# Turning attention outputs into columns on VectorE instead of TensorE, squaring on ScalarE, and three moved steps

## The chip, the cores and the metric

The kernel runs on one core of a Trainium2 chip. The metric is the device time of one execution in microseconds (us). Engines are named as in the profile: PE is TensorE (PEld its weight loads), DVE is VectorE, ACT is ScalarE, POOL is GpSimd, SP is SyncE, which issues most DMAs. Each engine works through its own queue in order, and waits at an instruction whose inputs are not there yet.

## The reference

The input `x` is 8 batches x 512 features x 1024 tokens, float32; a 0/1 mask says which tokens of a batch are kept. Eight heads of 64 features attend, with one projection for queries, keys and values, and the result is added to `x`:

```
xt = transpose(x, (0, 2, 1)); q = xt @ Wq.T              # per head: dk = 64
logits = (scale * q q^T * cmask + (1 - cmask) * -1e30) * rmask
attn = softmax(logits); ctx = attn @ q
out = transpose(ctx @ Wo.T, (0, 2, 1))
return x + out
```

A query that is masked has all its logits at 0, so it gets the mean over all tokens, which is the same for all masked queries.

## The kernel before

About half the tokens are kept. The kernel counts each batch's kept tokens and, if all have fewer than NK = 576, gathers them (and one row with the mean) into 576 columns, attends among those alone, multiplies by Wo, and spreads the rows back to 1024 tokens by an indirect DMA. A second path for all tokens stands behind a branch and does not run here.

**Tiles.** Features are cut into 4 pieces of 128 (a piece is two heads); a batch and a piece make a pair, so there are 8 x 4 = 32 pairs, `p` = 4b + pr. Keys are cut into 5 chunks (four of 128, one of 64). The main loop in `late` runs over pairs and in each over the chunks c = 0..4; such a step is called a slot (pr, c) here. The order of all engines' work is written out by hand: what a slot calls is recorded in that order, and each engine takes its instructions in it.

**A slot** does `scores` (PE: L625, two halves of two matmuls, PSUM tiles `s` in two buffers; ACT: the exponential L629 of each half), `add_up` of the chunk before (DVE: L646, sums over valid keys), then what the dictionaries and `slots_of` put there. After slot 4 comes `attend` (PE: L662, 40 matmuls; ACT copies the result, L678). Two pairs ahead, `project` (PE L556, 4 matmuls per half; ACT copy L563) and `values` (PE transposes L575, ACT copy L578, then DVE: square L583, sum by head L585, maximum L592) prepare queries and values. `bias_of` (L598) puts the maximum into a row with one PE product, reduces it on DVE (L600) and makes the bias that the next pair's exponentials need. It stands in slot 1. `contexts` (DVE, L750 to L759) scales a pair's result by inverse sums that went through DRAM (`row`, `rb`).

**Output of batch b.** During pair (b+1, 1), `output` (PE L775, ACT L782) multiplies by Wo in five pieces, put in slots 0, 1, 1, 2 and 3, and POOL stores them to DRAM (`od`, L784). `load_rest` in slot (1, 2) loads `x` again, as 8 tiles `xr` of 128 features x 512 tokens. `fetch` in slot (2, 0) has POOL gather rows of `od` by `origin` into 8 tiles `g` of 128 tokens x 512 features (L846). `finish`, two calls in each of the slots (3, 1) to (3, 4), makes 4 PE transposes (L858) into one PSUM bank and adds that to `xr` on DVE (L861); `issue_stores` issues the stores a slot later on SP (L863). The finish of batch 6 stands behind all of batch 7, and batch 7 itself has its own (`fetch_last` L835, `finish_tokens` L872, L873).

**Next batch's input.** In the slots (0, 2), (0, 4), (1, 0), (1, 1) DVE turns 32x32 blocks of the next `x` (L445; tiles `xt` in two buffers), and SP stores them as `xd` in DRAM (L453, four DMAs of 32 partitions each). `search` (L500) finds the kept tokens, `gather` in slot (1, 3) fetches them on POOL (L512), `collect` in slots (2, 2) and (2, 3) transposes them on PE (L525). `load_batch` in (3, 0) loads the batch after that.

**PSUM.** Two buffers of two banks hold `s`; every other product takes one of four banks in turn (`bank`), so a product waits until the reader of the fourth product before it is done.

Of the kernel before, what the change touches and what calls it, by code (L numbers as in the profile page):

```python
# [10 lines left out]
F32 = mybir.dt.float32  # L11
I32 = mybir.dt.int32
AF = mybir.ActivationFunctionType
ALU = mybir.AluOpType
# [7 lines left out]
Q = 32  # L22
# [296 lines left out]
def attention_of_kept_tokens(ctx, tc, x, mask, wq, wo, out, ident, wqT, woT, verdict, flag):  # L319
# [43 lines left out]
    sb = ctx.enter_context(tc.tile_pool(name="fsb", bufs=2))  # L363
# [7 lines left out]
    key = keep.tile([P, NC], F32, name="key")  # L371
    kept = keep.tile([P, B], F32, name="kept")
    origin = keep.tile([P, B, NT], I32, name="origin")
    pads = keep.tile([P, B, NC], F32, name="pads")
    pens = keep.tile([P, B, NC], F32, name="pens")
    low = keep.tile([P, 2, LAST], F32, name="low")
# [5 lines left out]
    def bank(name):  # L382
        return ps.tile([P, NB], F32, tag="t", name=name, bufs=4)
# [4 lines left out]
    stores = [[], []]  # L388
# [178 lines left out]
    def values(pair):  # L567
        nm = "%d_%d" % pair
        qT = qTs[pair]
        v = sb.tile([P, NC, P], F32, tag="v", name=f"v_{nm}", bufs=4)  # L570
        for at, n in ((0, LAST), (LAST, 1)):
            pt = bank(f"v_{nm}_{at}")
            for i in range(n):
                c = at + i
                nc.tensor.transpose(  # L575
                    pt[:, i * P : (i + 1) * P], qT[:, c * P : (c + 1) * P], ident
                )
            nc.scalar.copy(  # L578
                v[:, at : at + n, :], pt[:, : n * P].rearrange("p (c d) -> p c d", d=P)
            )  # L580
        vs[pair] = v
        sq = sb.tile([P, NC, P], F32, tag="sq", name=f"sq_{nm}", bufs=1)
        nc.vector.tensor_tensor(sq, v, v, ALU.mult)  # L583
        lengths = sb.tile([P, 2 * NC], F32, tag="len", name=f"len_{nm}")
        nc.vector.tensor_reduce(  # L585
            lengths,
            sq.rearrange("p c (h d) -> p (c h) d", h=2),
            axis=AX.X,
            op=ALU.add,
        )  # L590
        tops[pair] = sb.tile([P, 1], F32, tag="top", name=f"top_{nm}")
        nc.vector.tensor_reduce(tops[pair], lengths, axis=AX.X, op=ALU.max)  # L592
# [213 lines left out]
    def end_output(b, i):  # L806
# [12 lines left out]
        nc.vector.tensor_tensor(oc[:n, :], po[:n, :], partials[i][:n, :], ALU.add)  # L819
        nc.sync.dma_start(ods[b][places[i], :], oc[:n, :])  # L820

    def load_rest(b):
        for r in range(NN):
            for d in range(ND):
                xr = sb.tile([P, NB], F32, tag="xr", name=f"xr_{b}_{r}_{d}", bufs=NN * ND)
                nc.sync.dma_start(xr, x[b, d * P : (d + 1) * P, r * NB : (r + 1) * NB])
                xrs[b, r, d] = xr

    def fetch_last(b):

# [12 lines left out]
    def fetch(b):  # L843
        for i in range(NT):
            g = sb.tile([P, D], F32, tag="g", name=f"g_{b}_{i}", bufs=NT)
            nc.gpsimd.indirect_dma_start(  # L846
                out=g,
                out_offset=None,
                in_=ods[b],
                in_offset=bass.IndirectOffsetOnAxis(ap=origin[:, b, i : i + 1], axis=0),  # L850
            )
            gs[b, i] = g

    def finish(b, r, d):
        xr = xrs.pop((b, r, d))
        pt = bank(f"o_{b}_{r}_{d}")
        for i in range(G):
            nc.tensor.transpose(  # L858
                pt[:, i * P : (i + 1) * P], gs[b, r * G + i][:, d * P : (d + 1) * P], ident
            )  # L860
        nc.vector.tensor_tensor(xr, pt, xr, ALU.add)  # L861
        stores[0].append(
            lambda: nc.sync.dma_start(out[b, d * P : (d + 1) * P, r * NB : (r + 1) * NB], xr)  # L863
        )

    def finish_tokens(b, i):

# [18 lines left out]
    def slots_of(p):  # L886

        b, pr = pairs[p]
        todo = [[] for _ in range(NC)]
        if p + 2 < len(pairs):  # L890
            ahead = pairs[p + 2]
            at = (4, 4) if p == 2 else (3, 4) if pr == 2 else (1, 3) if p == 0 else (0, 2)
            for hf in range(2):
                todo[at[hf]].append(lambda hf=hf: project(ahead, hf))
            todo[LAST].append(lambda: values(ahead))
        if p == 0:
            behind = pairs[1]
            todo[0].append(lambda: project(behind, 1))
            todo[1].insert(0, lambda: values(behind))
            todo[3].insert(0, lambda: bias_of(behind))  # L900
        if p == ND - 1:
            for d in range(ND):
                todo[1 + d].append(lambda d=d: turn_weights(woT, "wo", d))
        if pr == 1 and b > 0:
            for i in range(NC):
                todo[(0, 1, 1, 2, 3)[i]].append(lambda i=i: output(b - 1, i))
        if pr == 2 and b + 1 < B:
            todo[1].append(lambda: put_mean(b + 1))
            for i in reversed(range(NC)):
                todo[(2, 2, 2, 3, 3)[i] + (b == 0)].insert(0, lambda i=i: collect(b + 1, i))  # L910
        if pr == 3 and 0 < b < B - 1:
            for i in range(NN * ND):
                r, d = divmod(i, ND)
                todo[1 + i // 2].append(lambda r=r, d=d: finish(b - 1, r, d))
        if p + 1 == len(pairs):
            for i in range(NC):
                todo[(1, 1, 2, 3, 4)[i]].append(lambda i=i: begin_output(b, i))
        return todo
# [29 lines left out]
    def early():  # L948
# [105 lines left out]
            search(0, i)  # L1054
        pt = bank("home_t")
        nc.tensor.transpose(pt[:, :BC], home, ident[:BC, :BC])
        nc.vector.tensor_copy(origin, pt[:, :BC].rearrange("p (b c) -> p b c", c=NT))

    def late():
        weights["wq"] = order_columns(load_weights(wq, "wq"), "wq")  # L1060
# [19 lines left out]
        TURN = [(0, 2), (0, 4), (1, 0), (1, 1)]  # L1080
        SEARCH = {(1, 0): (0, 1), (1, 1): (2,), (1, 2): (3,), (1, 3): (4,)}
        LATER = {(1, 1): (0,), (1, 2): (1,), (1, 3): (2, 3), (1, 4): (4,)}
        for p, pair in enumerate(pairs):
            b, pr = pair
            before = pairs[p - 1] if p else None
            todo = slots_of(p)
            for c in range(NC):
                scores(pair, c)
                if c:
                    add_up(pair, c - 1)  # L1090
                if c == 0 and before:
# [11 lines left out]
                if 0 < p < len(pairs) - 1 and c == (3 if p == 2 else 1):  # L1103
                    bias_of(pairs[p + 1])
                if b + 1 < B:
                    if (pr, c) in TURN:
                        turn(b + 1, TURN.index((pr, c)))
                    if pr < 2 and pr * NC + c < NN * ND:
                        add_features(b + 1, pr * NC + c)
                    if pr == 1 and c == 3:  # L1110
                        mean_of(b + 1)
                    for i in (SEARCH if b else LATER).get((pr, c), ()):
                        search(b + 1, i)
                    if pr == 0 and c == 1:
                        queries_of(b + 1)
                    if pr == 1 and c == (3 if b else LAST):
                        for i in range(NC):
                            gather(b + 1, i)
                if pr == 3 and c == 0 and b + 2 < B:
                    load_batch(b + 2)  # L1120
                    load_ranks(b + 2)
                if pr == 1 and c == 2 and b > 0:
                    load_rest(b - 1)
                if pr == 2 and c == 0 and b > 0:
                    fetch(b - 1)
                for task in todo[c]:
# [6 lines left out]
        attend_last(last)  # L1133
        for i in (0, LAST, *range(1, LAST)):
            end_output(B - 1, i)
        for r in range(NN):
            for d in range(ND):
                finish(B - 2, r, d)
                issue_stores()
# [113 lines left out]
```

## Time and profile before

| what | value |
|---|---|
| median of 3 runs | 738.48 us (737.36 to 738.85) |
| the profiled execution | 745.78 us, of which the span from first to last instruction is 744.1 us |
| mean granted PE clock | 0.981 |
| PE busy | 696.8 us (94%) |
| DVE busy | 526.8 us (71%) |
| ACT busy | 363.6 us (49%) |
| POOL busy | 171.0 us (23%) |
| moved by DMA | 117.40 MB, mean 158 GB/s |
| one batch in the middle, from `attend` to `attend` | 85 to 86 us |

The profile gives for each engine the time in which its instructions ran; a share near 100% doesn't say by itself that the engine sets the time. The chain of waits does: it is followed back from the last instruction, at each step to what released it. In the rows of instruction groups, the columns are line, engine, operation, what is written and read, shape, count | busy us in all, mean ns of one | idle us of the engine just before them and what ended it.

### The profile page before, as it was taken

Reading aid. Unit: us, or ns where it says so; the run is one execution under the profiler, and the core shown is the slowest. Engines: PE = TensorE matmul, PEld = TensorE weight load, DVE = VectorE, ACT = ScalarE, POOL = GpSimd, SP = SyncE. Lnnn points to the kernel's source line nnn. Section 1 sums busy time; section 2 is a strip of 40 time slices with the busy share of each in tenths; the row PEclk is TensorE's granted clock in tenths of the full one; section 3 lists DMA queues with packets and bytes.
Section 4 is the critical chain, followed back from the end, with each engine's and each line's share of the span. In section 5 each row is a group of like instructions: output and inputs, shape, how many; then the busy total and the mean of one; then the engine's idle time right before and its main releaser. Section 6 shows DMA issues by size and latency. Waiting matters only on the chain.

```text
span 744.1 us, 12368 instructions
## 1 busy us (share of the span) xinstructions
PE 696.8 (94%) x4251; PEld 405.1 (54%) x4251; DVE 526.8 (71%) x1527; ACT 363.6 (49%) x731; POOL 171.0 (23%) x208
## 2 busy tenths in 40 slices
PE   6799899999999899999999999999999999998983
PEld 5555565456655565456654565555654566554342
DVE  6279868774996569956897759956798668637462
ACT  5466466454553646345464546435473644435300
POOL 4712010161103501044101701044000620014021
PEclk9899999999999999999999999999999999999995
DMA  8544142754557463564738545574736542334047
GB/s 285 174 141 120 43 160 76 229 164 136 188 142 228 154 212 108 148 197 132 244 104 241 164 138 191 137 229 142 245 102 188 174 132 74 88 138 132 0 150 259
DMA packets 80857, 117.40 MB, mean 158 GB/s; under 512 B 10912, under 2 KB 43744, under 8 KB 80784
## 3 DMA queue, kind: packets, MB, share of 16 engines
q1 hardware_dynamic: 64032, 74.14, 32.3%
q0 software_dynamic: 12528, 40.28, 17.1%
q10 hardware_dynamic: 4224, 2.10, 1.0%
q8 instruction: 35, 0.57, 0.3%
q14 instruction: 38, 0.31, 0.1%
HBM read 73.30 MB, written 43.18 MB: 157 GB/s over the span
## 4 chain that ended last, share of the span: by engine, by line
PE 87%; ACT 4%; DVE 4%; DMA 2%; issue 1%; POOL 0%; another core or an unknown queue 0%; ACTq 0%; POOLq 0%; DVEq 0%
PE s L625 20%; PE av L662 20%; PE pq L556 18%; PE po L775 15%; PE o L858 3%; PE v L575 3%; ACT e L629 3%; PE xc L525 3%; PE pa L795 2%; DVE junk L500 1%; DMA g<-od,origin 1%; PE xt L416 1%; PE top L598 1%; DVE junk L646 1%; PE po L811 1%
## 5 line engine op out<-in xcount | busy, mean ns | idle before, releaser
L646 DVE CUSTOM_DVE_ANT_0 junk<-e,valid 128x576 f32<-128x576 f32 x256 | 193.3, 755 | 95.8 <-ACT e L629 90.0
L625 PE MATMUL s<-qT 64*128 64x288 f32 (+1 forms) x1280 | 185.1, 432 | 10.5 <-ACT e L629 10.4
L629 ACT ACTIVATE e<-s,bias 128x576 f32<-128x576 f32 x256 | 176.8, 739 | 35.5 <-PE s L625 30.0
L625 PEld LDWEIGHTS s<-qT 64*128 64x128 f32 (+1 forms) x1280 | 92.3, 174 | 91.9 <-issue 46.4
L556 PE MATMUL pq<-xc,wqT 128*128 128x288 f32 x512 | 140.5, 418 | 1.2 <-issue 1.2
L662 PE MATMUL av<-e,v 128*64 128x288 f32 x1024 | 134.1, 413 | 0.0
L556 PEld LDWEIGHTS pq<-xc,wqT 128*128 128x128 f32 x512 | 92.2, 190 | 42.2 <-issue 12.0
L775 PE MATMUL po<-woT,cT 128*128 128x512 f32 (+1 forms) x336 | 113.2, 523 | 0.0
L662 PEld LDWEIGHTS av<-e,v 128*64 128x64 f32 x1024 | 71.8, 138 | 51.1 <-issue 6.6
L784 POOL DMA_DIRECT2D od<-oc x42 | 24.0, 573 | 264.7 <-ACT oc L782 252.3
L678 ACT COPY cT<-av 128x288 f32<-128x288 f32 x62 | 21.8, 402 | 123.8 <-PE av L662 123.5
L775 PEld LDWEIGHTS po<-woT,cT 128*128 128x128 f32 (+1 forms) x336 | 49.8, 173 | 50.7 <-issue 46.2
L846 POOL DMA_INDIRECT g<-od,origin x56 | 61.8, 1104 | 34.2 <-PE s L625 11.9
L782 ACT COPY oc<-po 128x512 f32<-128x512 f32 (+1 forms) x35 | 19.0, 544 | 84.3 <-PE po L775 80.3
L583 DVE TENSOR_TENSOR sq<-v 128x640 f32<-128x640 f32 x32 | 26.0, 813 | 47.7 <-ACT v L578 46.2
L563 ACT COPY qT<-pq 128x288 f32<-128x288 f32 x64 | 25.6, 399 | 56.2 <-PE pq L556 51.4
L512 POOL DMA_INDIRECT xin<-xd,source x40 | 41.4, 1034 | 47.3 <-DVE cT L759 27.6
L404 POOL TENSOR_SCALAR valid<-count,kept 128x576 f32<-128x576 f32 x8 | 14.3, 1785 | 133.7 <-DVE sums L646 133.5
L861 DVE TENSOR_TENSOR xr<-o,xr 128x512 f32<-128x512 f32 x56 | 35.8, 684 | 7.7 <-PE o L858 7.3
L500 DVE TENSOR_SCALAR_CACHE_REDUCE junk<-rank,key 128x1024 f32<-128x1024 f32 (+4 forms) x40 | 39.7, 993 | 1.8 <-ACT rank L1025 1.8
L464 ACT ACTIVATE junka<-x 128x512 f32<-128x512 f32 x56 | 35.3, 631 | 0.0
L445 DVE STREAM_TRANSPOSE xt<-x 128x1024 f32<-128x1024 f32 x28 | 34.8, 1242 | 0.5 <-issue 0.2
(138 smaller groups left out, 651.4 us busy)
## 6 DMA issues: line engine op xcount, KB each, us to landing
x<-in_x_dram SPq DMA_DIRECT2D x56, 256.0 KB
xd<-xt SPq DMA_DIRECT2D x112, 128.0 KB
xr<-in_x_dram SPq DMA_DIRECT2D x56, 256.0 KB
out_dram<-xr SPq DMA_DIRECT2D x56, 256.0 KB
rb<-row SPq DMA_DIRECT2D x60, 160.0 KB
od<-oc POOLq DMA_DIRECT2D x28, 256.0 KB
rank<-ranks SPq DMA_DIRECT2D x6, 512.0 KB
xd<-xt POOLq DMA_DIRECT2D x8, 256.0 KB
```

The lines of the kernel that those rows point to most:

```text
L445: nc.vector.transpose(xt.rearrange("p k (d f) -> p k d f", d=ND), xs[b][r][:, :, at : at + n].rearrange("p d (k t) -> p k d t", t=Q),)
L464: nc.scalar.activation(junk, xs[b][r][:, d, :], AF.Copy, accum_out=xbars[b][:, d, r : r + 1])
L500: nc.vector.tensor_scalar(junk[:, :n], rank[:, i * P :], key[:, col], 0.0, ALU.is_le, ALU.add, accum_out=found[:, col])
L512: nc.gpsimd.indirect_dma_start(out=xin[:n, :], out_offset=None, in_=xds[b], in_offset=bass.IndirectOffsetOnAxis(ap=searches[b][2][:n, i : ...
L556: nc.tensor.matmul(pq[:, :KH], wqT[:, d, pr * P : (pr + 1) * P], xcs[b][:, d, cols], start=(d == 0), stop=(d == ND - 1),)
L625: nc.tensor.matmul(s[to, h, :KH], qT[heads[h], keys], qT[heads[h], queries], start=True, stop=True)
L629: nc.scalar.activation(e[:, hf if c < LAST else 0, :, :], s[:, :, :KH], AF.Exp, bias=biases[pair][:, c : c + 1], scale=SCALE,)
L646: nc.vector.tensor_tensor_reduce(junk[:, :n].rearrange("p (f k) -> p f k", k=KH), e[:, :, h, :], (valid if c < LAST else part).rearrange(" ...
L662: nc.tensor.matmul(av[head, :KH], v[keys, c, head], e[keys, hf if c < LAST else 0, h, :], start=(c == 0), stop=(c == LAST),)
L775: nc.tensor.matmul(po[k * n : (k + 1) * n, :w], cTs[b, pr][:, i * P : i * P + n], woT[:, pr, k * w : (k + 1) * w], start=(pr == 0), stop=( ...
L846: nc.gpsimd.indirect_dma_start(out=g, out_offset=None, in_=ods[b], in_offset=bass.IndirectOffsetOnAxis(ap=origin[:, b, i : i + 1], axis=0),)
L861: nc.vector.tensor_tensor(xr, pt, xr, ALU.add)
```

## The change

1. **Square.** `sq` in `values` is made by an ACT activation (Square) instead of a DVE product.
2. **Output into columns.** For all batches but the last, `finish` is replaced by `finish_blocks`. `x` and the output are seen as `(k f) (a n) -> a f k n` with f = 32 features and a = 4 quarters of the tokens: partition 32a + f holds the features f, 32 + f, 64 + f, ... of quarter a. `xr` becomes one tile of 128 x 16 x 256 in one buffer, loaded by four DMAs of 32 partitions with runs of 1 KB. Row 32a + t of gathered tile i is token 256a + 32i + t; `block_origin` holds the rows in that order and `place_blocks` makes it once in slot (2, 2) of batch 0, with 16 small DVE copies. `finish_blocks(b, i)` is then one DVE transpose of 32x32 blocks (128 x 512) and one DVE addition in SBUF, into 16 runs of 32. The output is stored by four DMAs, once per batch; for batch 6 in two halves.
3. **Where it stands.** The eight calls are in the slots (2, 3), (2, 4) twice, (3, 0) to (3, 3), and (0, 1) of the batch after; batch 6 has five calls in slots (3, 1) to (3, 3) of batch 7 and three behind it.
4. **Maxima.** `bias_of` moves from slot 1 to the slot of the pair's second projection (slot 2), for pr = 2 from slot 1 to slot 3.
5. **Output products.** The fifth piece of `output` moves from slot (1, 3) to slot (1, 2); so POOL stores it ahead of the five gathers and no longer behind them.

```diff
-        nc.vector.tensor_tensor(sq, v, v, ALU.mult)
+        nc.scalar.activation(sq, v, AF.Square)
...
+    def place_blocks():
+
+        for a in range(A):
+            for j in range(A):
+                nc.vector.tensor_copy(
+                    block_origin[a * Q : (a + 1) * Q, :, j::A],
+                    placed[j * Q : (j + 1) * Q, :, a * (NT // A) : (a + 1) * (NT // A)],
+                )
...
+        xr = sb.tile([P, D // Q, T // A], F32, tag="xr", name=f"xr_{b}", bufs=1)
+        for a in range(A):
+            nc.sync.dma_start(xr[a * Q : (a + 1) * Q, :, :], in_blocks(x[b])[a])
+        xrs[b] = xr
+
+    def finish_blocks(b, i):
+        o = sb.tile([P, D // Q, Q], F32, tag="o", name=f"o_{b}_{i}", bufs=2)
+        nc.vector.transpose(o.rearrange("p k t -> p (k t)"), gs[b, i])
+        xr = xrs[b]
+        to = xr[:, :, i * Q : (i + 1) * Q]
+        nc.vector.tensor_tensor(to, o, to, ALU.add)
+        n = NT if b + 2 < B else G
+        if (i + 1) % n == 0:
+            cols = slice((i + 1 - n) * Q, (i + 1) * Q)
...
+            stores[0].append(store)
...
-    def finish(b, r, d):
-        xr = xrs.pop((b, r, d))
-        pt = bank(f"o_{b}_{r}_{d}")
-        for i in range(G):
-            nc.tensor.transpose(
-                pt[:, i * P : (i + 1) * P], gs[b, r * G + i][:, d * P : (d + 1) * P], ident
-            )
-        nc.vector.tensor_tensor(xr, pt, xr, ALU.add)
...
+            if 0 < p != 2:
+                todo[at[pr != 2]].append(lambda: bias_of(pairs[p + 1]))
...
-                todo[(0, 1, 1, 2, 3)[i]].append(lambda i=i: output(b - 1, i))
+                todo[(0, 1, 1, 2, 2)[i]].append(lambda i=i: output(b - 1, i))
...
+        FINISH = {
+            (2, 3): (0,),
+            (2, 4): (1, 2),
+            (3, 0): (3,),
+            (3, 1): (4,),
+            (3, 2): (5,),
+            (3, 3): (6,),
+            (0, 1): (7,),
+        }
+        FINISH_LAST = {(3, 1): (0, 1), (3, 2): (2, 3), (3, 3): (4,)}
```

More of the change, by code (lines that the diff above doesn't have):

```diff
@@ L373, in attention_of_kept_tokens @@
     origin = keep.tile([P, B, NT], I32, name="origin")
+    placed = keep.tile([P, B, NT], F32, name="placed")
+    block_origin = keep.tile([P, B, NT], I32, name="block_origin")
     pads = keep.tile([P, B, NC], F32, name="pads")
@@ L820, in end_output, with in_blocks, store @@
         nc.sync.dma_start(ods[b][places[i], :], oc[:n, :])
-    def load_rest(b):
[L823 to L827, printed above, removed]
+    BLOCKS = range(B - 1)
+    def place_blocks():
[5 more added lines that the diff above has]
+                )
+    def in_blocks(t):
+        return t.rearrange("(k f) (a n) -> a f k n", f=Q, a=A)
+    def load_rest(b):
+        xr = sb.tile([P, D // Q, T // A], F32, tag="xr", name=f"xr_{b}", bufs=1)
[11 more added lines that the diff above has]
+            cols = slice((i + 1 - n) * Q, (i + 1) * Q)
+            def store():
+                for a in range(A):
+                    nc.sync.dma_start(
+                        in_blocks(out[b])[a][:, :, cols], xr[a * Q : (a + 1) * Q, :, cols]
+                    )
+            stores[0].append(store)
     def fetch_last(b):
@@ L849, in fetch @@
                 in_=ods[b],
-                in_offset=bass.IndirectOffsetOnAxis(ap=origin[:, b, i : i + 1], axis=0),
+                in_offset=bass.IndirectOffsetOnAxis(
+                    ap=block_origin[:, b, i : i + 1], axis=0
+                ),
             )
             gs[b, i] = g
-    def finish(b, r, d):
-        xr = xrs.pop((b, r, d))
-        pt = bank(f"o_{b}_{r}_{d}")
-        for i in range(G):
-            nc.tensor.transpose(
-                pt[:, i * P : (i + 1) * P], gs[b, r * G + i][:, d * P : (d + 1) * P], ident
-            )
[L861 to L864, printed above, removed]
     def finish_tokens(b, i):
@@ L910, in slots_of @@
                 todo[(2, 2, 2, 3, 3)[i] + (b == 0)].insert(0, lambda i=i: collect(b + 1, i))
[L911 to L914, printed above, removed]
         if p + 1 == len(pairs):
@@ L1056, in early @@
         nc.tensor.transpose(pt[:, :BC], home, ident[:BC, :BC])
-        nc.vector.tensor_copy(origin, pt[:, :BC].rearrange("p (b c) -> p b c", c=NT))
+        nc.vector.tensor_copy(placed, pt[:, :BC].rearrange("p (b c) -> p b c", c=NT))
+        nc.vector.tensor_copy(origin, placed)
     def late():
@@ L1102, in late @@
                     contexts(before)
-                if 0 < p < len(pairs) - 1 and c == (3 if p == 2 else 1):
+                if (p, c) in ((2, 3), (len(pairs) - 2, 1)):
                     bias_of(pairs[p + 1])
@@ L1125, in late @@
                     fetch(b - 1)
+                if p == 2 and c == 2:
+                    place_blocks()
+                for i in (FINISH if b + 1 < B or pr == 0 else FINISH_LAST).get((pr, c), ()):
+                    of = b - 2 if pr == 0 else b - 1
+                    if of in BLOCKS:
+                        finish_blocks(of, i)
                 for task in todo[c]:
@@ L1135, in late @@
             end_output(B - 1, i)
[L1136 to L1139, printed above, removed]
+        for i in range(5, NT):
+            finish_blocks(B - 2, i)
+        issue_stores()
         worst = sb.tile([P, 2], F32, tag="worst", name="worst")
```

## The prediction

> **What bounds the kernel now.** I read the chain of waits first, by engine and then, for one middle batch, in order of time; after that the groups by shape, for durations, and the windows, for DMA. On the page the chain is PE's:
>
> ```profile
> PE 87%; ACT 4%; DVE 4%; DMA 2%; issue 1%; POOL 0%; another core or an unknown queue 0%; ACTq 0%; POOLq 0%; DVEq 0%
> PE s L625 20%; PE av L662 20%; PE pq L556 18%; PE po L775 15%; PE o L858 3%; PE v L575 3%; ACT e L629 3%; PE xc L525 3%; PE pa L795 2%; DVE junk L500 1%; DMA g<-od,origin 1%; PE xt L416 1%; PE top L598 1%; DVE junk L646 1%; PE po L811 1%
> ```
>
> So work taken from PE shortens the run, and work given to DVE or ACT costs nothing until its lateness reaches PE. The transposes to be removed (L858) have 3% of the chain. In order of time, with start, length and what ran, pair 3 and the pair 0 after it read:
>
> ```profile
> 431.29 4.68 PE av L662 x40
> ...
> 440.70 0.87 PE o L858 x8
> ...
> 444.88 0.87 PE o L858 x8
> ...
> 446.93 1.02 PE o L858 x8
> ...
> 449.29 0.87 PE o L858 x8
> 450.17 4.68 PE av L662 x40
> ...
> 458.15 0.71 PE s L625 x4
> ...
> 458.94 0.75 ACT e L629
> ...
> 459.74 1.39 PE s L625 x8
> ...
> 463.26 0.71 PE s L625 x4
> ...
> 464.00 0.75 ACT e L629
> ...
> 464.79 0.72 PE s L625 x8
> 465.50 0.70 PE v L575 x5
> 466.20 4.03 PE av L662 x31
> ```
>
> The reader is to see two things. Pair 3 takes 18.88 us (431.29 to 450.17), 3.63 of it `o`. Pair 0 takes 16.04 us (450.17 to 466.20), has the same PE work without `o`, and there the chain leaves PE twice for an exponential: a slot with scores alone takes PE 1.17 us and ACT 2 x 0.74 us, and two PSUM buffers don't hide that.
>
> The rows that give the prices:
>
> ```profile
> L861 DVE TENSOR_TENSOR xr<-o,xr 128x512 f32<-128x512 f32 x56 | 35.8, 684 | 7.7 <-PE o L858 7.3
> L464 ACT ACTIVATE junka<-x 128x512 f32<-128x512 f32 x56 | 35.3, 631 | 0.0
> L445 DVE STREAM_TRANSPOSE xt<-x 128x1024 f32<-128x1024 f32 x28 | 34.8, 1242 | 0.5 <-issue 0.2
> ```
>
> **PE, pair 3 (batches 1 to 6).** Without `o` its PE work is pair 0's, so I take pair 0 as its measure, not the 3.63 us: where `o` stood, PE now waits for exponentials. Pair 0's 16.04 us hold the maxima's product (`top`, 0.25 us) for nothing, since it runs inside the first wait. The change moves it behind the projection, where PE is full: 16.29 us. 18.88 - 16.29 = 2.59 us, x 6 = **-15.5 us**. The ends: all 3.63 us go (-21.8), or every scores-only slot waits as in batch 7's pair 2, where the chain is on ACT (two exponentials and 0.28 us of hand-over, 1.65 us against 1.17): four slots lose 0.48 us, 3.63 - 1.9 = 1.7, -10.3.
>
> **PE, what is moved.** `top` out of its gap costs pair 0 of batches 1 to 7 0.25 us each, +1.75, and pair 3 of batch 0 +0.25; in pairs 1 and 2 it finds full slots before and after. The fifth output piece (1.88 us) stood between the scores of slots (1, 3) and (1, 4) and hid the exponential. Without it that stretch is 0.71 (half the scores) + 0.08 + 0.75 (exponential) + 0.04 + 0.72 = 2.30 us against 1.17 + 0.65 = 1.82: +0.48 x 7 = +3.4. Together **+5.4 us** (0 if other work fills these gaps).
>
> **ACT.** L583 took 813 ns on DVE. By L464, ACT's nearest row, 128x640 costs 631 + 128 x 0.83 = 0.74 us. It stands behind the copy of `v`, ahead of `attend`; there ACT waits for PE anyway (123.5 us over 31 waits of the copy L678, 4 us each). So nothing, in 31 places; in the prologue it replaces the DVE square on the path, even. Without that cover: 0.74 x 32 = 24 us. The Trainium skill ("ScalarE: Activation LUTs", Rules for kernel authors) says to keep products on VectorE, and (What ACT_TABLE_LOAD costs) that a function outside the loaded set costs 2.66 us per switch. By that rule 64 switches would cost ACT 170 us and the change would lose. But the trace has one table load, and the changed program's instruction order still has one, ahead of all exponentials. I take the row.
>
> **DVE.** `finish_blocks` is a transpose of 512 (L445 has 1.24 us for 1024, the 128x32 transpose L732 0.21; in between, 0.71) and an addition as L861, 0.68; back to back they overlap by some 0.07 each: 1.25 us, against 0.60 (two L861 took 1.28 with their ends overlapping). A batch gets 8 x 1.25 - 8 x 0.60 - 4 x 0.83 = +1.9 us on 65 us in 85. It is local lateness that matters. Finish 0 to 2 fall into pair 2's idle stretch (4.47 us ahead of L583). From 438.2, the first exponential of pair 3, DVE then runs without a gap: six chunks added 9.3, finishes 4 to 7 5.0, bias 0.65, `contexts` 2.25, lengths 0.95, last chunk 0.95, inverses 1.35, turn 1.2, waits 1.0: 22.6 us, so the reduction L600 of pair 0 comes at 460.8. PE puts its `top` at 460.5 (2.6 us earlier than now) and, four banks on, `attend` needs that bank at 463.6: 2.8 us to spare. Pair 3's bias has about the same, and DVE catches up in pair 1, where it idles 4 us at the exponential of (1, 3). Cost taken: 0. The addition's runs of 32 have no row: not less than 0.60 us, as elements are as many; above, twice, 1.3. The transpose: 0.62 (half of L445) to 1.24.
>
> **Queues.** SP: eight loads and eight stores become four and four. The store leaves the time of the `x` load (3, 0) and comes as one burst of 2.1 MB in (0, 2), ahead of the first `xd` store; behind it on SP wait the `xd` stores, and for these DVE's third turn in (1, 0), 13 us after the burst starts, as `xt` has two buffers; then `gather`. The Trainium skill ("SBUF — State Buffer", Door 1) speaks against it: 32 partitions reach half of the ports, 189 GB/s against 328 at 1 MiB. The nearest row, four `xd` stores of 32 partitions and 0.52 MB in one 2.5 us window, says 206:
>
> ```profile
> 385.00:387.50 2.50, 2.50 (x14) 1.74 (x13) 2.33 (x11) 2.50 (x6) 0.00 (x0) 1.00 0.85 206
> 447.50:450.00 2.50, 2.50 (x26) 1.82 (x23) 2.49 (x6) 1.76 (x4) 0.00 (x0) 1.00 1.02 402
> ```
>
> The second row is 128 partitions. Burst and first `xd` store, 2.6 MB, need 12.7 us by the row and 13.9 by the rule: DVE may wait 1 to 3 us in (1, 0), inside pair 1's idle time. I take 0; as `gather` has some 8 us behind the last `xd` store, about 10 us of delay are free. POOL: the fifth piece's store goes ahead of the gathers, which start 1.5 us later (8 issues of some 1.25 us behind them start 1.5 us earlier, as they no longer wait for that store); the last gathered chunk is issued at 416 instead of 415 and needed at 422.9. Nothing.
>
> **Batch 0.** Its second half hangs on DVE (chain, 60 to 80 us); a square of 0.81 us goes and a wait for `top` of 0.3: **-1.0**. The 16 copies (as L759, 0.15 us: 2.4 us) come behind that, ahead of a bias that is ready at 87.4 and needed at 92.8; uncovered they cost 2.4.
>
> **The end.** DMA shares from 718 to 740 us are 0.85 to 1.15: stores of batch 6 (2.1 MB), gathers, and stores of batch 7 compete. Half of batch 6 now leaves earlier: 1.05 MB at 320 GB/s are 3.3 us less; the eight gathers' issue, until 728.3, allows most of it. I take **-2.5** (0 to -3.5).
>
> **Sum.** -15.5 + 5.4 - 1.0 - 2.5 = **-13.6 us**: 745.78 becomes 732.2. That execution lies 1% above the median of the runs; from 738.48 the same step leads to **725**.
>
> **Rivals.** (a) *ACT takes over in pair 3*: -10.3 in place of -15.5, the rest as above, -8.4: **730**. For it: ACT ends two waits of pair 0. Against: ACT has 9.2 us of work in pair 3 (window 172 to 191), of 16.3. (b) *DVE late, PE waits at the bank of `top`* (slower): its place is `attend` of pair 0. It decides once the four finishes ahead of it cost 2.8 us more than forecast, so from 1.95 us for one; at the upper ends (1.24 + 1.3 = 2.54) they cost 5.2 more, PE waits 2.4 us in each of 7 batches, 16.8 less 13.6: **742**. For it: no idle time on DVE from (3, 1) on. Against: both durations lie between rows. (c) *The burst of stores delays `xd`, gather and `collect`*: the 2.6 MB may take 12.7 + 10 us, 115 GB/s; at 100 they take 26, PE waits 3.3 us in (2, 2) of six batches, 20 less 13.6: **745**; at 105 no change. For it: the rule. Against: the row has twice that rate. (d) *The gaps stay full* (all 3.63 us gained, nothing for moved steps, -25.3 with the rest): **713**.
>
> **Chances.** Forecast 0.58, (a) 0.17, (d) 0.06, (b) 0.11, (c) 0.08. A measurement here tells 0.2%, 1.5 us, from no change. Slower takes (b) and most of (c), no change some of (c) and the slow edge of (a). The range 716 to 738 takes in (a) and leaves out (b), most of (c) and (d); the likeliest case alone has 720 to 729, from its ends at the end of the run (0 to -3.5) and 0.25 us a pair for the waits.
>
> **What would show it.** Right: pair 3 takes about 16.3 us from `attend` to `attend`, pair 1 about 31.3, L858 gone, ACT's square 0.74 us ending before L678. Wrong: idle time of `av` or `top` on PE ended by DVE (b), of `xc` ended by a DMA or of the turn L445 by `xd` (c), more chain on L629 than now (a), a `finish_blocks` over 1.95 us, or more than one table load.

## The result, and the profile after

| | median | lowest to highest | runs |
|---|---|---|---|
| before | 737.92 us | 737.16 to 738.85 | 4 |
| changed | 727.61 us | 726.34 to 728.51 | 4 |

The ratio is 0.9859, 95% interval [0.9835, 0.9882]: 10.3 us less, where 13.5 were forecast (725). The profiled execution of the changed kernel took 726.34 us (span 724.6), the lowest of its four. Of the runs told of below, four (before_again, m_back, out_back, both_back) were made while PE's signals reached ACT late, and the kernel before read 747.1 us (741.21 to 751.11) beside them; these four are read pair by pair, not by their medians.

The changed kernel's lines are two further down: L625 is now L627 (scores), L629 is L631 (exponential), L598 is L600 (`top`), L600 is L602 (its reduction) and L662 is L664 (`attend`). The chain of waits of the changed kernel, by engine and by line:

```profile
PE 82%; DVE 7%; ACT 6%; DMA 3%; issue 2%; POOL 0%; SPq 0%; DVEq 0%; POOLq 0%
PE av L664 19%; PE s L627 19%; PE pq L558 17%; PE po L777 15%; ACT e L631 4%; PE v L577 3%; PE xc L527 2%; DVE junk L648 2%; PE pa L797 2%; DVE junk L502 1%; DMA g<-od,origin 1%; PE xt L418 1%; DMA rb<-row 1%; PE po L813 1%; PE top L600 0%
```

`o` is gone from it, PE still sets the time, and DVE has 7% in place of 4%. The same chain in order of time (start, length, what ran), pair 3 and pair 0 of a batch in the middle:

```profile
419.19 4.83 PE av L664 x40
424.01 1.17 PE s L627 x8
425.19 2.14 PE pq L558 x8
427.32 0.71 PE s L627 x4
...
428.06 0.75 ACT e L631
...
432.37 0.11 PE top L600
...
433.21 0.75 ACT e L631
...
435.42 0.64 PE av L664 x4
436.06 0.00 issue
436.06 4.26 PE av L664 x36
...
448.68 0.11 PE top L600
```

Pair 3 (419.19 to 435.42) takes 16.23 us for 18.88, and looks like pair 0 now: the two exponentials that `o` had hidden stand in the chain. That is why 2.6 us came of the 3.6 that were removed. `top` stands behind the projection with 0.11 us, and `attend` takes 4.90 us (0.64 + 4.26) where it took 4.68. The groups by shape (count | busy us, mean ns of one | idle before):

```profile
L846 DVE STREAM_TRANSPOSE o<-g 128x512 f32<-128x512 f32 x56 | 39.3, 701 | 0.0
L849 DVE TENSOR_TENSOR xr<-o,xr 128x512 f32<-128x512 f32 x56 | 38.8, 692 | 1.9
L585 ACT ACTIVATE sq<-v 128x640 f32<-128x640 f32 x32 | 23.6, 737 | 1.0
L447 DVE STREAM_TRANSPOSE xt<-x 128x1024 f32<-128x1024 f32 x28 | 34.7, 1240 | 11.0 <-DMA xd<-xt 10.9 <-issue 0.2
```

The three new operations cost 701, 692 and 737 ns; taken were 0.71, 0.68 and 0.74 us. The last row is the burst of stores: DVE's turn of the next `x` now waits 10.9 us in all for earlier `xd` stores.

From `attend` to `attend`, in us. "Before" is batch 5, where nothing was disturbed:

| pair | before | changed | forecast |
|---|---|---|---|
| 3 | 18.87 | 16.23 | 16.29 |
| 0 | 16.04 | 16.31 | 16.29 |
| 1 | 30.84 | 31.32 | 31.32 |
| 2 | 18.87 | 19.09 | 18.87 |
| a batch | 84.62 | 82.95 | 82.77 |

The first profile of before held 7.3 us more than that (so do the 85 to 86 us a batch of the table of the time before): its pair 2 took 20.38, 21.02, 19.26, 20.25 and 19.08 us in batches 1 to 4 and 6, and one pair 3 20.56. This is what its 745.78 us lie above the median (738.48). Without it the spans compare as 736.7 to 724.6: pair 3 -2.64 x 6, pair 0 +0.27 x 6, pair 1 +0.48 x 7, pair 2 +0.22 x 5, batch 0 -0.5, the other pairs of batch 7 -0.5, the end -1.4, together -12.1. Medians say 10.3, as the changed kernel's profile is 1.3 us below its median and the corrected one of before 0.5 above.

### The profile page after: what moved, and what is told of

Its sections match the earlier page's. It is cut to its first block, busy times and chain, and to the rows that moved or that the text cites. A ratio compares the mean times of both kernels' runs of the same rounds, so it can differ in the third digit from the quotient of the medians.

```text
span 724.6 us, 11742 instructions
## 1 busy us (share of the span) xinstructions
PE 673.4 (93%) x4027; PEld 378.0 (52%) x4027; DVE 542.0 (75%) x1568; ACT 384.1 (53%) x763; POOL 171.9 (24%) x208
## 4 chain that ended last, share of the span: by engine, by line
PE 82%; DVE 7%; ACT 6%; DMA 3%; issue 2%; POOL 0%; SPq 0%; DVEq 0%; POOLq 0%
PE av L664 19%; PE s L627 19%; PE pq L558 17%; PE po L777 15%; ACT e L631 4%; PE v L577 3%; PE xc L527 2%; DVE junk L648 2%; PE pa L797 2%; DVE junk L502 1%; DMA g<-od,origin 1%; PE xt L418 1%; DMA rb<-row 1%; PE po L813 1%; PE top L600 0%
## 5 line engine op out<-in xcount | busy, mean ns | idle before, releaser
L627 PE MATMUL s<-qT 64*128 64x288 f32 (+1 forms) x1280 | 186.7, 434 | 16.9 <-ACT e L631 16.7
L631 ACT ACTIVATE e<-s,bias 128x576 f32<-128x576 f32 x256 | 175.5, 737 | 20.4 <-PE s L627 17.2
L627 PEld LDWEIGHTS s<-qT 64*128 64x128 f32 (+1 forms) x1280 | 91.7, 174 | 103.9 <-ACT e L631 50.2
L664 PE MATMUL av<-e,v 128*64 128x288 f32 x1024 | 135.8, 411 | 0.1
L664 PEld LDWEIGHTS av<-e,v 128*64 128x64 f32 x1024 | 69.6, 136 | 55.0 <-ACT v L580 8.3
L879 POOL DMA_INDIRECT g<-od,block_origin x56 | 62.1, 1109 | 19.0 <-issue 14.3
L514 POOL DMA_INDIRECT xin<-xd,source x40 | 42.4, 1060 | 43.8 <-DVE m L603 25.6
L447 DVE STREAM_TRANSPOSE xt<-x 128x1024 f32<-128x1024 f32 x28 | 34.7, 1240 | 11.0 <-DMA xd<-xt 10.9
L587 DVE TENSOR_REDUCE len<-sq 128x10 f32<-128x640 f32 x32 | 25.8, 806 | 21.3 <-ACT sq L585 21.3
L849 DVE TENSOR_TENSOR xr<-o,xr 128x512 f32<-128x512 f32 x56 | 38.8, 692 | 1.9
L846 DVE STREAM_TRANSPOSE o<-g 128x512 f32<-128x512 f32 x56 | 39.3, 701 | 0.0
```

The source lines that it names most:

```text
L447: nc.vector.transpose(xt.rearrange("p k (d f) -> p k d f", d=ND), xs[b][r][:, :, at : at + n].rearrange("p d (k t) -> p k d t", t=Q),)
L514: nc.gpsimd.indirect_dma_start(out=xin[:n, :], out_offset=None, in_=xds[b], in_offset=bass.IndirectOffsetOnAxis(ap=searches[b][2][:n, i : ...
L627: nc.tensor.matmul(s[to, h, :KH], qT[heads[h], keys], qT[heads[h], queries], start=True, stop=True)
L631: nc.scalar.activation(e[:, hf if c < LAST else 0, :, :], s[:, :, :KH], AF.Exp, bias=biases[pair][:, c : c + 1], scale=SCALE,)
L664: nc.tensor.matmul(av[head, :KH], v[keys, c, head], e[keys, hf if c < LAST else 0, h, :], start=(c == 0), stop=(c == LAST),)
L846: nc.vector.transpose(o.rearrange("p k t -> p (k t)"), gs[b, i])
```

## The experiments

"DVE" and "PE" lines keep the changed kernel's numbers unless said. Where a median is compared, the changed kernel is 727.32 us (after_again) and before 737.8 to 738.0 beside it.

### Before and after once more

No edit. First before, alone:

> The kernel before, unchanged, profiled a second time. In its first profile pair 2 of batches 1 to 4 took 19.26 to 21.02 us against 18.87 in batch 5, about 7.4 us in all, which is just what that execution (745.78) lies above its median. Theory (chance): in another execution pair 2 takes 18.87 us in all of batches 1 to 5 and the whole is 737 to 739 us. Rival (built in: the store of the fifth piece behind the gathers, or the eight stores and loads of x, delay something in pair 2): the same batches are again 0.4 to 2 us longer, and the median holds some of that, so part of the gain of the change is its removal.

It took 754.22 us. Pair 2 of batches 1 to 3 took 21.34, 21.05 and 21.32 us, 18.97 and 18.99 in batches 4 and 5. So the same pair is disturbed again, which speaks against chance alone, but not in every batch. How it comes about is seen in the first profile of before, on the timeline (start, length, engine, line; in brackets the idle time ahead and what ended it):

```profile
252.79 1.07 POOL L846 DMA_INDIRECT g<-od,origin  x1 [0.30 <-remote]
254.65 0.40 ACT L563 COPY qT<-pq 128x288 f32<-128x288 f32 x1 [1.79 <-PE s L625]
256.10 0.74 ACT L629 ACTIVATE el<-s,bias 128x576 f32<-128x576 f32 x1 [1.05 <-PE pq L556]
257.59 0.40 ACT L563 COPY qT<-pq 128x288 f32<-128x288 f32 x1 [0.75 <-remote]
258.05 0.55 PE L575 MATMUL v<-ident,qT 128*128 128x128 f32 x3 [2.42 <-ACT qT L563]
```

PE had ended that projection at 255.40; its signal came at 257.57, while POOL issued the gathers of `fetch`. ACT starts late, and PE loses 2.4 us.

> The changed kernel, unchanged, beside the next run. Theory (a property of the order): its pair 2 takes 19.1 us in batches 2 to 6 again, without idle time of PE over 0.7 us there, and the whole is 726 to 729 us on any chip. Rival (a property of the chip the last runs used, where before read 747 instead of 738): on a chip where before reads over 741, its pair 2 also grows to 20 to 21 us in some batches or, as in m_back, to 31.

727.32 us (727.24 to 728.35), ratio 0.9857 [0.9836, 0.9878], pair 2 at 19.08 to 19.09 in batches 2 to 6. Before read 737.8 here, so these runs were undisturbed and the rival was not put to the test.

### The maxima's product back in slot 1

```diff
-            if 0 < p != 2:
-                todo[at[pr != 2]].append(lambda: bias_of(pairs[p + 1]))
...
-                if (p, c) in ((2, 3), (len(pairs) - 2, 1)):
+                if 0 < p < len(pairs) - 1 and c == (3 if p == 2 else 1):
```

> The changed kernel with one part undone: the maxima's product and bias_of stand in slot 1 again. The prediction's term: 0.25 us in pair 0 of batches 1 to 7 and in pair 3 of batches 0 to 6, about 3.5 us, comes back: 724.1 us against 727.6, pairs 0 and 3 at 16.05 us. Rival 1: only the 0.11 us that the chain shows for this product comes back, 1.5 us: 726. Rival 2 (the move was needed): DVE comes late to the reduction with the finishes in its queue, the attend that takes the product's bank waits, over 728 us, with idle time of av or v on PE ended by DVE.

809.9 us (808.95 to 811.24), ratio 1.0834 [1.0804, 1.0863]. Pairs 0 and 3 took 15.98 us as expected, but pair 2 took 31.4 to 32.7 in every batch. The timeline at the start of one of them:

```profile
253.57 1.24 PE L627 MATMUL s<-qT 64*128 64x288 f32 x8
254.91 0.96 POOL L879 DMA_INDIRECT g<-od,block_origin  x1 [0.30 <-issue]
255.64 0.40 ACT L680 COPY cT<-av 128x288 f32<-128x288 f32 x1 [5.39 <-PE s L627]
...
259.25 0.74 ACT L631 ACTIVATE e<-s,bias 128x576 f32<-128x576 f32 x1 [1.74 <-remote]
260.04 1.33 PE L627 MATMUL s<-qT 64*128 64x288 f32 x4 [5.24 <-issue]
262.79 0.74 ACT L631 ACTIVATE e<-s,bias 128x576 f32<-128x576 f32 x1 [2.80 <-PE s L627]
```

All eight score products had ended at 254.81, yet the second exponential starts at 262.79. In the changed kernel's profile the signals of the same products came 0.02 to 0.04 us after their ends; here they came at 259.23 and 262.77, with POOL's eight gathers running beside. PE was also granted less clock. The rows show windows of 4 us: busy time (and instructions) of PE, PEld, DVE, ACT and POOL, then the granted PE clock, the DMA share and GB/s:

```profile
248.00:252.00 4.00, 4.00 (x35) 2.32 (x33) 3.11 (x9) 2.12 (x4) 3.37 (x3) 1.00 0.83 222
...
256.00:260.00 4.00, 0.00 (x0) 0.00 (x0) 0.00 (x0) 1.18 (x3) 2.91 (x4) 0.92 0.63 203
...
268.00:272.00 4.00, 4.00 (x17) 2.96 (x18) 2.57 (x7) 2.46 (x4) 0.00 (x0) 0.50 0.00 0
```

The clock reads 0.50 from 259.3 to 273.0 us, and for 13.7 to 17.1 us in pair 2 of each of batches 1 to 6; eight score products that take 1.24 us at 253.57 take 2.29 at 267.81. So it is the disturbance of before, some 12 to 14 us long in place of 2, and made longer by the clock. Whether it belongs to this order of work was asked next:

> The kernel with bias_of back in slot 1, a second time. It took 809.9 us instead of the 724 that the prediction's term gives; all of the loss was in pair 2 (31 to 32 us for 19), where PE's completion signals reached ACT 2 to 8 us late while POOL issued its eight gathers. Theory (order): again 805 to 815 us, wherever it runs, with pair 2 over 30 us in every batch. Rival (chip): on another chip 722 to 727 us, with pairs 0 and 3 at 15.98 us and pair 2 at about 19.

The same file took 725.29 us (721.99 to 727.07), ratio 0.9833 [0.9803, 0.9864], pair 2 at 18.75. The records give the same chip for both, so it was neither the order alone nor another chip. The spans of the two profiles differ by 88.5 us: 28.0 of them are busy time of PE (700.0 us against 672.0, for as many products), which ran longer at the lower clock, and 60.5 its idle time. In the profile (721.99 us) a batch takes 81.98 us, 0.97 less than with the move: pair 0 -0.33, pair 3 -0.26, pair 2 -0.33, pair 1 -0.05. The chain shows where: `attend` and the two waits are there, `top` is not, as it runs inside the first wait.

```profile
335.29 4.68 PE av L664 x40
339.97 1.17 PE s L627 x8
341.14 2.14 PE pq L558 x8
343.28 0.71 PE s L627 x4
...
344.01 0.75 ACT e L631
```

The prediction's 0.25 us for a moved `top` is thus 0.11 in its place and 0.15 to 0.22 in `attend`, whose first products take longer. The chain of the changed kernel breaks at the fifth product of `attend`, where turn_twice, below, shows a wait for the reader of `top`'s bank (the reduction L602 on DVE); that this wait costs some time even when it was fulfilled long ago is argued from there, not shown. By the medians 2.0 us came back, by the profile 5.3; what the longer of these four runs held was not recorded.

### The fifth output piece back in slot (1, 3)

```diff
-                todo[(0, 1, 1, 2, 2)[i]].append(lambda i=i: output(b - 1, i))
+                todo[(0, 1, 1, 2, 3)[i]].append(lambda i=i: output(b - 1, i))
```

> The changed kernel with one part undone: the fifth piece of the output product stands in slot (1, 3) again. The prediction's term: 0.48 us in pair 1 of batches 1 to 7, 3.4 us, comes back: 724.2 us, pair 1 at 30.84 us. Rival (the move was needed): the piece's store stands behind five gathers on POOL and delays the fetch, the finishes 0 to 2 in pair 2 or the collect come later, and pair 2 or 3 grows by as much: 727 to 729 us.

734.25 us (727.24 to 741.08), one of the four disturbed measurements. Pair 1 took 30.89 us in its profile (0.43 less), pairs 0 and 3 16.31 and 16.24 as in the changed kernel, pair 2 19.14 to 21.33, PE waiting up to 2.1 us for a late copy of `qT`. Of the term of 0.48 us 0.43 came back; the rival's delay can't be told from the disturbance here. Both steps back at once:

> The changed kernel with both moved steps undone (bias_of in slot 1, fifth piece in slot (1, 3)); what stays is the turn on VectorE and the square on ScalarE. The prediction's terms add: 3.5 + 3.4 less, 720.7 us; a batch in the middle takes about 82.95 - 0.98 = 82.0 us. Rival: the two gaps are used by the same work, or DVE's lateness shows once PE is faster, and the sum is smaller than the two alone: 723 or more.

730.38 us, disturbed like out_back: pair 2 took 19.0 to 20.7. Once more, beside an undisturbed kernel before:

> Both moved steps undone (bias_of in slot 1, fifth piece in slot (1, 3)), a second time: in its first measurement the kernel before, beside it, read 747.1 us in place of 738 and the runs spread over 10 us. The prediction's terms: 3.5 us for the maxima and 3.4 us for the piece come back, 720.4 us where the changed kernel has 727.3. By the undisturbed pairs of its first profile: 81.84 us a batch against 82.95, x 6 to 7, 720. Rival: undone, POOL's fetch falls less well, pair 2 grows in some batches and the median is 723 or more.

720.91 us (719.70 to 723.25), ratio 0.9764 [0.9749, 0.9779], 6.4 us under the changed kernel; a batch takes 81.55 us, pairs 15.97, 15.97, 30.85 and 18.75. The rival (723 or more) is out. The turn on VectorE and the square on ScalarE alone are worth 17 us; the two moved steps give 6.4 of them back.

The 6.4 us are a balance. A batch in the middle gains 1.40 us, but batch 0 loses 3.0: its pairs 2 and 3 take 21.49 and 18.81 us where after_again has 20.12 and 17.13. There PE waits 1.33 us for the reduction L602, which now stands on DVE behind the 16 copies of `place_blocks`, and from 88.4 to 91.8 us the granted PE clock reads 0.50. So the maxima's move did help batch 0: by 1.4 to 3.0 us with the copies there (m_back_again, with the product alone moved back, takes 21.48 and 17.13), and by 1.0 with the copies elsewhere (20.06 us for pair 2 in the last experiment, 19.08 in place_later).

### How much DVE work is covered

```diff
         nc.vector.transpose(o.rearrange("p k t -> p (k t)"), gs[b, i])
+        nc.vector.transpose(o.rearrange("p k t -> p (k t)"), gs[b, i])
```

> The changed kernel with every DVE transpose of finish_blocks made twice into the same tile (56 more of 0.70 us, 39 us more on DVE). One finish then costs 1.35 + 0.72 = 2.07 us. The prediction put the point from which DVE decides at 1.95 us for one finish (2.8 us to spare for four): by it PE loses 4 x 0.12 = 0.5 us in pair 0 of 7 batches, 3 us, 731 us. Rival 1 (DVE has more cover than that): no change, 728. Rival 2 (rival b of the prediction, DVE is at its limit already): four finishes cost 2.9 us more in each of 7 batches, 20 us, 748, with idle time of av on PE ended by DVE.

750.94 us (746.90 to 755.89), ratio 1.0195 [1.0151, 1.0239]: 23.6 us lost where the prediction's point gives 3 and rival 2 gives 20. The timeline of one pair 0:

```profile
455.21 0.15 DVE L761 COPY cT<-qT 128x1 f32<-128x1 f32 x1
455.46 0.40 ACT L565 COPY qT<-pq 128x288 f32<-128x288 f32 x1 [2.07 <-DVE cT L761]
456.55 1.39 PE L627 MATMUL s<-qT 64*128 64x288 f32 x8 [1.40 <-ACT e L631]
464.64 0.25 DVE L602 TENSOR_REDUCE m<-top 128x1 f32<-128x128 f32 x1
464.94 2.40 PE L664 MATMUL av<-e,v 128*64 128x288 f32 x18 [1.18 <-DVE m L602]
```

There are two places at which PE waits. The later one is the one foreseen: the bank of `top` (L602). The earlier one was not: `contexts` (L761) is the last reader of an old `qT`, ACT's copy into that buffer waits for it, and the exponentials behind that copy come late. In the changed kernel L761 ends together with `attend` (440.27 against 440.32), here 4.7 us behind it (455.36 against 450.67). Seven finishes between slot (2, 3) and there, 0.74 us longer each, make 5.2. So the finishes in pair 2 count too. Against the changed kernel's first profile, the pairs 0 take 10.1 us more in all (5.2 of them in batch 4), the pairs 1, which hold the waits at the bank, 5.9, and the end, from pair 3 of batch 7 on, 4.5. The changed kernel's timeline of DVE says why; this is the only idle time of DVE that the view marks between 419.9 and 452:

```profile
429.46 0.76 DVE L648 CUSTOM_DVE_ANT_0 junk<-e,valid 128x576 f32<-128x576 f32 x1 [0.39 <-ACT e L631]
```

The corrected sum (eight finishes, some 3 us to spare at the bank: L602 ends at 449.12, the fifth product of `attend` comes at 452.1) was then tested between the two:

```diff
+        nc.vector.transpose(o.rearrange("p k t -> p (k t)")[:, : 12 * Q], gs[b, i][:, : 12 * Q])
```

> The changed kernel with a second DVE transpose of 384 of the 512 columns in every finish_blocks: one finish costs 1.35 + 0.59 = 1.94 us. The prediction's point is 1.95 us for one finish (four count): 727 to 728 us. The corrected sum after turn_twice (DVE runs without a gap from slot (2, 3) to (0, 2), so all eight finishes count, 3.2 us to spare): 8 x 0.59 = 4.7 us, 1.5 us too late in each of 7 batches, and the end some 3 us later by its own three finishes: 739 to 742 us.

741.04 us (740.01 to 743.46), ratio 1.0053 [1.0032, 1.0074]. The waits of PE in its profile (total, times, longest):

```profile
PE s L627 <- ACT e L631: 21.9, 48, 4.7
...
PE av L664 <- DVE m L602: 4.2, 4, 1.2
```

The prediction's point (727) does not hold: PE waits at the very bank that it named. The time lies where the corrected sum put it (739 to 742), but its parts do not, so that size is in part luck. PE waited at the bank in four batches and not in seven, which makes the pairs 1 longer by 5.1 us in all, where the sum had 10.5, and the end by 0.8, where it had 3. Half of the loss, 6.6 us, is one pair: pair 0 of batch 4 takes 22.87 us for 16.31, with the wait of 4.7 us for an exponential (first row). DVE had stood still for 6.0 us in pair 2 of batch 3 (1.2 in the changed kernel) until the inverse sums were back from DRAM, and reached L761 some 4 us later than in the other batches. The chain of turn_part has these transfers:

```profile
326.35 5.21 DMA row<-rt
...
332.19 6.04 DMA rb<-row
```

From 368.1 to 374.9 us the granted PE clock then read 0.50. Why the transfers were slow in that batch was not followed up. What stays is that the finishes in pair 2 count and that the cover is some 3 us. The square back on DVE:

```diff
-        nc.scalar.activation(sq, v, AF.Square)
+        nc.vector.tensor_tensor(sq, v, v, ALU.mult)
```

> The changed kernel with one part undone: the square is a DVE product again (0.81 us), ACT has no square. The prediction costs the square on ACT at nothing and counts its gain at nothing outside batch 0 (-0.5 to -1). From turn_twice, DVE has some 3.2 us until its lateness reaches PE in pair 0, and two squares (1.6 us) come into that stretch: so nothing there, 727 to 728.5 us. Rival (ACT's square is what makes the finishes fit on DVE): DVE is late by more than 3.2 us, 1 to 2 us in each of 7 batches, 735 to 741.

730.42 us (729.83 to 731.98), ratio 0.9904 [0.9885, 0.9923]: 3.1 us lost, between the theory and its rival. PE's waits:

```profile
PE av L664 <- DVE m L602: 1.8, 2, 1.1
```

These two waits are in batch 0 (1.1 us) and batch 4. In the profile, against after_again, 1.1 us are lost in batch 0, where the square stands on the path; 1.2 in pairs 3 and 0, which take 16.36 and 16.37 us in place of 16.23 and 16.31, where the exponentials that PE waits for come up to 0.07 us later each; and 0.9 in batch 4, where DVE came late to the bank after a wait of 4.7 us for the inverse sums in pair 2 of batch 3. So about a third is the gain in batch 0, and the square on ACT is part of DVE's cover too, but at its edge: it showed at the bank in one batch of seven.

### The copies of place_blocks out of batch 0

```diff
-                if p == 2 and c == 2:
+                if p == 5 and c == 4:
                     place_blocks()
```

> The changed kernel with place_blocks (16 small DVE copies) in slot (1, 4) of batch 1, before its first reader, instead of slot (2, 2) of batch 0. Theory: in batch 0 the copies are on the path; without them pair 2 of batch 0 is 1 to 3 us shorter (36.3 down to 34), and in pair 1 of batch 1 DVE waits for exponentials anyway: 725 to 726.5 us. Rival: batch 0 is bound by something else just behind the copies and nothing comes back, 727.6; or they now delay the maxima of (1, 4), 729.

725.66 us (725.58 to 727.25), ratio 0.9837 [0.9814, 0.9860]. The chain of the changed kernel (its second profile) holds the copies, with DVE behind them:

```profile
80.54 0.08 DVE block_origin L830
...
83.43 0.03 issue
83.46 0.76 DVE junk L648
...
87.22 0.21 DVE m L602
```

Without them, the chain of place_later leaves DVE for the inverse sums' way through DRAM:

```profile
79.94 2.99 DMA rb<-row
...
85.23 0.21 DVE m L602
```

Pairs 1 and 2 of batch 0 (from its first `attend` to its third) take 35.17 us together, where after_again has 36.20, the changed kernel's first profile 36.26 and before 36.80. The expectation took these 36.3 us for pair 2 alone, and its 34 was not reached. Of the 3 us of copies 1.0 came back there, 1.7 by the medians; the DMA is next in line.

### All together

Both moved steps undone, place_blocks in (1, 4), and the last three finishes of batch 6 ahead of the end:

```diff
-        FINISH_LAST = {(3, 1): (0, 1), (3, 2): (2, 3), (3, 3): (4,)}
+        FINISH_LAST = {(3, 1): (0, 1), (3, 2): (2, 3), (3, 3): (4, 5)}
...
         inv = inverses(pair)
+        finish_blocks(B - 2, 6)
...
                     sum_last(pair)
+                    finish_blocks(B - 2, 7)
+                    stores[0].pop()(nc.scalar)
```

> The changed kernel with both moved steps undone (-7 us), place_blocks in slot (1, 4) of batch 1 (-1.6), and the last three finishes of batch 6 ahead of the end: finish 5 in slot (3, 3), 6 and 7 in attend_last, where DVE waits for PE 2.7 and 2.1 us, and its second store issued by ACT there, while DMA has nothing to do. The end loses 4 us of DVE work ahead of the last check and 1.05 MB of stores behind it: -3. Sum 715.5 us. Rival 1: the finishes delay the last context and its output products by as much, and the store delays the od stores: 719. Rival 2: the end is bound by the eight gathers and the last stores alone: 718.

720.95 us (719.35 to 722.41), ratio 0.9772 [0.9754, 0.9791]: beats both kernels, but is no better than both_back_again (720.91). In its profile the last `attend` starts 4.0 us earlier than in that of both_back_again (680.29 against 684.33), 3.1 of them from batch 0 and 2.0 from pair 3 of batch 7, less 1.0 by which its first `attend` came later. That pair took unusually long in both_back_again: 28.40 us, where all other profiles but those of before_again and turn_twice have 25.6 to 26.9. The end takes 1.4 back, 38.5 us from there for 37.1. What is left of the difference is not in the medians: the profiled execution of both_back_again was the slowest of its five (723.25). The chain of best at the end:

```profile
686.68 3.87 PE po L816 x8
690.55 3.98 DMA od<-oc
```

and the timeline of what met the `od` store:

```profile
685.60 3.20 ACTq L859 DMA_DIRECT2D out_dram<-xr  x4
688.49 4.35 SPq L825 DMA_DIRECT2D od<-oc  x5
```

The megabyte that was moved out of the end now travels with the `od` stores. An `od` store takes 3.98 us to land (2.56 on the chain of before), and the first gather is issued 3.1 us after the last output product (691.51 to 694.66), 1.1 us in both_back_again. The output products themselves come no later: the last ends 11.2 us after the start of `attend` in both. So it is the second half of rival 1, the store; that the two stores slow each other is read from their times alone. Without this last edit the parts add up to some 718 to 719 us; that was not run.

## Why the prediction was right, point by point

- **PE, pair 3.** Forecast 16.29 us, measured 16.23. Taking pair 0 as the measure, and not the 3.63 us of `o`, was the step that mattered: rival (d), all 3.63 us gained, would have given 713, and by (a) pair 3 would have taken 17.2. The pair holds the moved `top` as well: with `top` back in slot 1 it takes 15.97, as pair 0 does.
- **PE, what is moved.** `top` in pair 0: +0.25 forecast, +0.27 measured. That the size fits is luck: the 0.25 us were the product's length, and it stands in the chain with 0.11; the rest is a longer `attend`, which the prediction did not have. Fifth piece: +0.48, and +0.48. "In pairs 1 and 2 it finds full slots before and after" failed in pair 2: 19.09 us, and 18.75 with the product back in slot 1. That is 0.22 x 5 = 1.1 us of the 3.2 that the forecast missed by. Pair 3 of batch 0 lost nothing (17.13 both times), where 0.25 was forecast.
- **ACT.** 0.737 us against 0.74, hidden. "So nothing" holds for what it costs ACT. The 0.83 ns for an element come out of the trace of before: its copies L782 of 512 and of 256 elements take 586 and 373 ns. The trace has one table load, as forecast. But the square's gain was put at nothing outside batch 0, and of the 3.1 us that sq_back lost some two thirds lie outside it: without it DVE's cover is at its edge.
- **DVE.** One finish takes 1.35 us, not 1.25: the addition follows 0.74 us after the transpose starts, and the next operation 0.61 after it. It stayed hidden, as forecast, and the spare time at the bank was right (some 3.0 us against 2.8). The point from which it decides was wrong: 1.95 us for one finish counted four finishes, but DVE has no pause of weight from (2, 3) on, so all eight count. turn_part at 1.94 us for one lost 13.7 us where 0 was forecast, 5.1 of them with waits at the bank. Rival (b) was nearer than its 0.11 said: 3 us of cover over eight finishes are 0.4 us for each.
- **Queues.** The turn in (1, 0) was forecast to wait 1 to 3 us for `xd`; the longest of six waits was 2.7, inside the idle time named. The row of 206 GB/s and the 189 GB/s of the Trainium skill ("SBUF — State Buffer", Door 1) both led there, and no transfer reached PE through `gather`.
- **Batch 0.** Forecast -1.0. From its first `attend` to that of pair 2 it took 36.26 us in the first profile and 36.20 in the second, before 36.80: -0.5 to -0.6. "The 16 copies come behind that" failed: they stand ahead of the last sums and `contexts` on DVE. Without them it is 35.17, so -1.6: the term was too small, and the copies, put at nothing, took 1.0 of it.
- **The end.** Forecast -2.5, measured -1.4 from the last `attend` on (36.4 us for 37.8; after_again has 37.3). The term counted the stores that leave earlier and left out that finishes 5 to 7 of batch 6 stand on DVE ahead of the last check, which they hold back from 700.1 to 704.2 us.
- **Scale.** The sum was made from 745.78 and carried to the median. That was needed: the changed kernel's profile lies 19.4 us lower, 7.3 of them a disturbance that the change did not remove by design. The terms measured in the profiles add up to -12.1 us where -13.6 were forecast; the other 1.8 us to the measured 10.3 are the distances of the two profiles from their medians, and no term of the sum.
- **Signs.** Two of the signs named for being wrong came without their rivals: ACT's exponential has 4% of the chain in place of 3% (a), and the turn waited for `xd` (c). The forecast itself held both, with two exponentials in each pair 3 and 1 to 3 us in (1, 0), so they could not tell it from its rivals; the length of the pairs could.

## What to carry to other kernels

Work taken off a bound engine is worth what the next wait leaves of it: take a stage that lacks this work as the measure, not the instructions' own sum. A spare time found at one place must be divided by all the work that has come in since the engine last stood idle, and every buffer that its instructions free is a place to look. And before a small step is moved "behind something longer", see whether it runs inside a wait now; if so, moving it costs time that it did not cost there: here 0.11 us in its new place and 0.15 to 0.22 in the product behind it, for a step of 0.25.

## What was not expected of the hardware

While POOL issued its train of indirect gathers, PE's completion signals came up to 8 us after the modelled end of the products (0.02 to 0.04 us at other times), with DMA at 0.6 to 0.8 of its share in those stretches. The Trainium skill ("Perfetto Trace Analysis", Summary: the profiler window per engine type) says that TensorE's end is an estimate and that the travel of semaphore updates is not in the window; so the trace doesn't tell whether the products or their signals were late. The same file took 809.9 us once and 725.29 another time, and about a third of that (28.0 of 88.5 us between the profiles) was not the lateness itself but products that ran longer while the granted PE clock read 0.50. What sets this off stays open: it came in both profiles of before, in one series of runs and not in two others, mostly in pair 2, where `fetch` runs. A kernel without these gathers, or with them in another slot, was not tried.
